# One-hot matrices turned by one product and two activations, and a target's scores taken in one product of 12 columns

## The chip, the cores and the metric

The kernel runs on one core of one Trainium2 chip. The metric is the device time of one execution, in microseconds (us); shorter is better. It is written by hand with a tile framework that allocates buffers, sets semaphores and orders the instructions of each engine.

## The reference

A graph of 6250 nodes with 256 features and 100,000 edges (`src`, `dst`, sorted by `dst`) passes through four layers of message passing. After each there is a residual addition and a layer norm.

```python
x = _layernorm(x + _L0_gnn_ref(x, ...))   # mean over incoming edges of relu(norm(x))[src]; two 256x256 products
x = _layernorm(x + _L1_gnn_ref(x, ...))   # 8-head attention: softmax over the edges of one src of q[src].k[dst], sum of v[dst]
x = _layernorm(x + _L2_gnn_ref(x, ...))   # two GAT layers, 4 heads of 64, below; gelu after each
x = _layernorm(x + _L3_gnn_ref(x, ...))   # mean over incoming edges of x[src]; three products
...
# one GAT layer
h = (h_in @ W).reshape(n, Hh, Cc)
alpha_s = jnp.sum(h * a_s, axis=-1)
alpha_d = jnp.sum(h * a_d, axis=-1)
e = jax.nn.leaky_relu(alpha_s[src] + alpha_d[dst], 0.2)
m = jax.lax.stop_gradient(jax.ops.segment_max(e, dst, num_segments=n))
ex = jnp.exp(e - m[dst])
alpha = ex / jax.ops.segment_sum(ex, dst, num_segments=n)[dst]
out = jax.ops.segment_sum(h[src] * alpha[:, :, None], dst, num_segments=n)
```

In the third step each node also has an edge to itself. A value that belongs to an edge's target, such as `alpha_d[dst]`, has to be brought from the node to each of its edges; the sums go the other way, from the edges to the node.

## The kernel before, in words

**Tiling.** The nodes are cut into `NB` = 50 blocks of `B` = 125. The edges of a block are laid in a list of up to `CAP` = 2048 places, 16 columns (`CM`) of 128 edges; what doesn't fit goes to two more columns (`SH`) that ten blocks (`GB`) share. For each place there is the number of the node at the far end (`idx_d`, `idx_s`) and a key, the place of the near node in its block (`key_d` for lists by target, `key_s` for lists by source). Both lie with the 128 edges of a column on the partitions. The lists by target are made first by `by_target` (L928), from the sorted `dst`; those by source by `by_source` (L1257), in small steps beside the first layer.

**A pass.** Each layer is a pass over pieces: a piece is four columns of one block (six in the first and last layer). For each column `gather` (L881) issues one indirect DMA on the POOL queue, which fetches 128 rows of a table in DRAM into the tile `g`. The sum over the edges of a node is a product on PE: the one-hot matrix `st` (128 edges by 125 nodes, made by VectorE in `one_hots`, L886, by comparing keys with `iota_p`) times the messages (L1755, L1955, L911).

**Where the change sits.** To bring a value from node to edge the turned matrix `ts` (125 nodes by 128 edges) is wanted as PE's stationary operand. `turned_hots` (L897) makes it: four transposes on PE of f32 (L901) into one PSUM tile `tp`, then one copy by ScalarE to bf16 (L903). Two passes use it:

- `piece1` (L1715), the attention pass over lists by source, 200 pieces: `ts` times the node's q, held as three bf16 parts, makes `qe` (L1739); VectorE multiplies it by the gathered k (L1742), sums over a head (`s`, L1687), ScalarE takes Exp (L1691, L1692), VectorE scales v into `msg` (L1694), PE adds into the block's sums `ps` (L1755).
- `piece2` (L1905), a GAT layer over lists by target, 200 pieces in each of two layers: `ts` times `ad_parts`, the node's four scores held as three bf16 parts, makes `pe` (L1922), three products of four columns for each of four columns of edges, added in PSUM. Then `messages` (L1880): VectorE adds gathered and own score (`e`, L1883), takes the leaky relu (`r`, L1877), ScalarE takes Exp (`pp`, L1886), VectorE makes `msg` (L1889), PE adds (L1955). Beside these pieces `count_edges` (L1780) builds a matrix of edge counts for the last layer, with VectorE (`a_hot`, L1804), PE (L1826) and ScalarE (`a_row`, L1813).

**Order of the work.** `run_pass` (L1490) starts one piece at each step and advances every piece that is under way by one `yield`, so about ten pieces are in flight, at different stages. After the last piece of a block `finish1` or `finish2` normalises, multiplies by weights, and writes the block's rows of the next layer's table on the SP queue (`move`, L795). The next pass's gathers read that table, so they start when all 50 blocks have been written: there is a seam between each two passes. `g` has 7 buffers in the attention pass and 9 in the GAT layers; `ts` 3, `msg` 3, `pe` and `pp` one each; `tp` one in the attention pass and two in the GAT layers. Engines run their queues in order; the framework sets the order from the order in which the code issues, its own estimates and free buffers. Only in the first stage, up to the writing of `h_table_f` (L1104), is the order on VectorE, ScalarE, POOL and SP that of the code (`manual_schedule`).

Of the kernel before, what the change touches and what calls it, by code (L numbers as in the profile page):

```python
# [7 lines left out]
F32 = mybir.dt.float32  # L8
I32 = mybir.dt.int32
F16 = mybir.dt.float16  # L10
BF16 = mybir.dt.bfloat16
AF = mybir.ActivationFunctionType
ALU = mybir.AluOpType
AX = mybir.AxisListType
ENG = mybir.EngineType

P = 128
# [638 lines left out]
def gnn_stack_kernel(ctx: ExitStack, tc: tile.TileContext, ins, out):  # L656
# [13 lines left out]
    nc = tc.nc  # L670
# [4 lines left out]
    B = max(p for p in range(1, P + 1) if N % p == 0)  # L675
    NB = N // B
    CM, SH = -(-E // (NB * P)), 2
# [4 lines left out]
    CAP = CM * P  # L682
# [19 lines left out]
    for c in range(EC):  # L702
        g = c // GQ
# [12 lines left out]
    for r in range(NR):  # L716
# [4 lines left out]
        c0 = max(0, int(place_of(g0 * GQ * EQ, -1)) // P) if g0 else 0  # L721
# [18 lines left out]
    with ExitStack() as fast:  # L740
        const = fast.enter_context(tc.tile_pool(name="fconst", bufs=1))
        dram = fast.enter_context(tc.tile_pool(name="fdram", bufs=1, space=bass.MemoryType.DRAM))
# [5 lines left out]
        pidx = const.tile([P, 1], F32, name="pidx")  # L748
        nc.gpsimd.iota(pidx, pattern=[[1, 1]], base=0, channel_multiplier=1, allow_small_or_imprecise_dtypes=True)
        ident = const.tile([P, P], F32, name="ident")  # L750
        nc.vector.tensor_scalar(ident, diff, 0.0, None, op0=ALU.is_equal)
        ones = const.tile([P, P], F32, name="ones")
        nc.vector.memset(ones, 1.0)
        ident_b = const.tile([P, P], BF16, name="ident_b")
# [24 lines left out]

        edge_rows = dram.tile([ER, P], I32, name="edge_rows_f")  # L780
        q_table = dram.tile([N, 3 * D], BF16, name="q_table_f")
        kv_table = dram.tile([N, 2 * D], F32, name="kv_table_f")
# [113 lines left out]

        def turned_hots(work, psum, st, n, bufs):  # L897

            tp = psum.tile([B, 4, P], F32, name="tp", bufs=bufs)
            for i in range(n):  # L900
                nc.tensor.transpose(tp[:, i, :], st[:, i, :], ident)  # L901
            ts = work.tile([B, 4, P], BF16, name="ts", bufs=3)
            nc.scalar.copy(ts[:, :n, :], tp[:, :n, :])  # L903
            return ts
# [23 lines left out]
        def by_target(pool, psum):  # L928
# [69 lines left out]
            for v, o in ((f, idx_d), (k_f, key_d)):  # L998
                for c0 in range(0, CM, 10):
# [4 lines left out]
                    nc.scalar.copy(o[:, :, c0 : c0 + n], pt[:, :n, :].rearrange("p i b -> p b i"))  # L1004
            yield
            p_row = psum.tile([1, NB + 1], F32, name="p_row")
            nc.tensor.transpose(p_row, row, ident[: NB + 1, : NB + 1])
# [635 lines left out]
        with tc.tile_pool(name="f1g", bufs=7) as gp, tc.tile_pool(name="f1", bufs=1) as pool, tc.tile_pool(  # L1643
# [71 lines left out]
            def piece1(b, c0, n):  # L1715
# [14 lines left out]
                yield  # L1730
                ts = turned_hots(work, psum, st, n, 1)
                yield
# [26 lines left out]
                if c0 + n == CM:  # L1759
                    del held[b]  # L1760
                    yield
                    yield from finish1(b)


# [72 lines left out]
        for layer in range(2):  # L1837
            table = hs_tables[layer]
            with tc.tile_pool(name=f"f2{layer}", bufs=1) as pool, tc.tile_pool(
# [5 lines left out]
                w_gat = gat_weight(pool, work, 1) if layer == 0 else None  # L1845
                sums, held, shared, late = {}, {}, {}, []

                def finish2(b):
# [56 lines left out]
                def piece2(b, c0, n):  # L1905
# [10 lines left out]
                    yield  # L1916
                    ts = turned_hots(work, psum, st, n, 2)
                    yield
                    pe = psum.tile([P, 4, H2], F32, name="pe")
                    for i in range(n):  # L1920
                        for k in range(3):
                            nc.tensor.matmul(  # L1922
                                pe[:, i, :], ts[:, i, :], ad_parts[:, b, k, :], start=(k == 0), stop=(k == 2)
                            )
                    yield
                    msg = work.tile([P, 4 * H2, C2 + 1], F32, name="msg", bufs=3)
                    steps = messages(g, n, pe[:, :n, :], msg)
                    next(steps)
# [238 lines left out]
```

## Time and profile before

| what | value |
|---|---|
| time, median of 3 runs | 7063.73 us (7057.86 to 7067.16) |
| the profiled execution's own time | 5192.17 us |
| its span | 5190.3 us |
| mean granted TensorE clock | 0.931 |
| busy PE / VectorE / ScalarE / POOL | 80% / 70% / 39% / 72% |
| gathers of the five passes | 800, 800, 800 + 800, 544 |
| first layer (lists made, h_table_f gathered) | 0 to 1249 us |
| attention pass, first to last gather of kv_table_f | 1235 to 2287 us |
| two GAT layers, first to last gather of hs_table_f | 2371 to 4450 us |
| last layer, from its first gather | 4474 to 5190 us |

A profile is one execution recorded by the hardware. Its own time lies well under the times of the runs that were not profiled, while span and own time agree; durations below are those of the profile. PE is TensorE's products, PEld its loads of the stationary operand, DVE is VectorE, ACT ScalarE, POOL GpSimd (here it issues the gathers), SP the queue of the plain DMAs. A group's line gives the source line, engine, operation, output and inputs, shapes and count; then the busy time in us and the mean of one in ns; then the idle time of the engine just before, with what ended most of it. "issue" is idle time that no recorded wait explains.

### The profile page before, as it was taken

Reading aid. Unit: us, or ns where it says so; the run is one execution under the profiler, and the core shown is the slowest. Engines: PE = TensorE matmul, PEld = TensorE weight load, DVE = VectorE, ACT = ScalarE, POOL = GpSimd, SP = SyncE. Lnnn points to the kernel's source line nnn. Section 1 sums busy time; section 2 is a strip of 40 time slices with the busy share of each in tenths; the row PEclk is TensorE's granted clock in tenths of the full one; section 3 lists DMA queues with packets and bytes.
Section 4 is the critical chain, followed back from the end, with each engine's and each line's share of the span. In section 5 each row is a group of like instructions: output and inputs, shape, how many; then the busy total and the mean of one; then the engine's idle time right before and its main releaser. Section 6 shows DMA issues by size and latency. Waiting matters only on the chain. (4 is left out here: it accounts for less than half of the span.)

```text
span 5190.3 us, 84722 instructions
## 1 busy us (share of the span) xinstructions
PE 4167.6 (80%) x27626; PEld 3130.5 (60%) x27626; DVE 3645.6 (70%) x11269; ACT 2029.7 (39%) x5923; POOL 3762.6 (72%) x3889
## 2 busy tenths in 40 slices
PE   0457999997999999976887888877777777799996
PEld 0245667665777777754666666655556656466664
DVE  7576788765999999975666666657777777423434
ACT  4011898895222222222444444434444444211212
POOL 6677677766777777745777777767777777677776
PEclk9877899998999999987999999989989899899998
DMA  4556677666777777753544444444444444788875
GB/s 132 147 156 175 174 194 191 187 171 189 224 224 227 224 224 227 225 148 101 136 131 131 133 131 137 131 114 135 133 133 136 135 136 134 201 244 245 246 208 144
DMA packets 365014, 883.97 MB, mean 170 GB/s; under 512 B 83596, under 2 KB 181954, under 8 KB 364562
## 3 DMA queue, kind: packets, MB, share of 16 engines
q0 software_dynamic: 232032, 702.40, 49.3%
q1 hardware_dynamic: 132530, 176.06, 11.5%
q8 instruction: 220, 3.60, 0.3%
q14 instruction: 232, 1.90, 0.1%
HBM read 791.50 MB, written 86.63 MB: 169 GB/s over the span
## 5 line engine op out<-in xcount | busy, mean ns | idle before, releaser
L882 POOL DMA_INDIRECT g<-hs_table_f,idx_d x1600 | 1528.8, 956 | 487.3 <-issue 424.0
L882 POOL DMA_INDIRECT g<-h_table_f,idx_d x800 | 795.6, 994 | 297.8 <-issue 210.8
L1955 PE MATMUL ps<-msg,st 128*125 128x260 f32 x3200 | 875.6, 417 | 83.4 <-DVE msg L1889 45.6
L882 POOL DMA_INDIRECT g<-kv_table_f,idx_s x784 | 744.0, 949 | 250.6 <-issue 184.6
L911 PE MATMUL ps<-g,st 128*128 128x256 bf16 (+1 forms) x4032 | 634.8, 282 | 201.1 <-DMA g<-h_table_f,idx_d 98.0
L1955 PEld LDWEIGHTS ps<-msg,st 128*125 128x125 f32 x3200 | 635.8, 204 | 232.6 <-issue 50.1
L882 POOL DMA_INDIRECT g<-x_table_f,idx_d x544 | 516.0, 949 | 189.1 <-issue 152.9
L903 ACT CAST ts<-tp 125x512 bf16<-125x512 f32 x600 | 347.5, 579 | 728.0 <-PE tp L901 709.9
L911 PEld LDWEIGHTS <-st 128*128 128x128 bf16 x4536 | 444.9, 101 | 295.5 <-issue 190.1
L1889 DVE TENSOR_TENSOR msg<-g,pp 128x1024 f32<-128x1024 f32 x400 | 485.3, 1213 | 19.7 <-ACT pp L1886 18.3
L1883 DVE TENSOR_TENSOR e<-g,pe 128x16 f32<-128x16 f32 x400 | 68.3, 171 | 607.3 <-DMA g<-hs_table_f,idx_d 419.6
L1755 PE MATMUL ps<-msg,st 128*125 128x264 f32 x1600 | 406.5, 396 | 51.1 <-DVE ln_t L825 12.9
L891 DVE TENSOR_TENSOR st<-iota_p,key_d 128x500 f32<-128x500 f32 (+1 forms) x550 | 410.0, 746 | 44.7 <-PE ps L911 27.0
L1922 PEld LDWEIGHTS <-ts 125*128 125x128 bf16 x4800 | 178.0, 97 | 430.7 <-issue 333.9
L1922 PE MATMUL pe<-ad_parts,ts 125*128 125x4 bf16 x4800 | 178.2, 165 | 320.3 <-DVE e L1883 255.5
L901 PE MATMUL tp<-ident,st 128*125 128x128 f32 x2400 | 405.5, 292 | 35.2 <-DVE st L891 16.1
L901 PEld LDWEIGHTS tp<-ident,st 128*125 128x125 f32 x2400 | 343.8, 197 | 67.1 <-issue 25.9
L1755 PEld LDWEIGHTS ps<-msg,st 128*125 128x125 f32 x1600 | 288.4, 190 | 113.9 <-issue 41.7
L1826 PE MATMUL a_acc<-a_hot,a_st 128*128 128x500 f16 x950 | 300.1, 403 | 38.7 <-ACT a_row L1813 28.0
L1739 PE MATMUL qe<-q,ts 125*128 125x256 bf16 x2400 | 311.2, 274 | 21.7 <-DVE prod L1742 9.9
L1438 ACT ACTIVATE oa<-o,blk 125x128 f16<-125x128 f16 x800 | 312.2, 391 | 38.9 <-PE acc L1445 28.6
L1804 DVE TENSOR_SCALAR a_hot<-a_nodes,a_ends 128x500 f16<-128x500 f16 x950 | 321.0, 364 | 1.9 <-PE a_acc L1826 1.4
(428 smaller groups left out, 8229.4 us busy)
## 6 DMA issues: line engine op xcount, KB each, us to landing
g<-hs_table_f,idx_d POOLq DMA_INDIRECT x1600
a_table_f<-a_row SPq DMA_DIRECT2D x50, 437.5 KB
cnt<-a_table_f SPq DMA_DIRECT2D x50, 437.5 KB
xs<-x_table_f SPq DMA_DIRECT2D x50, 336.0 KB
g<-h_table_f,idx_d POOLq DMA_INDIRECT x800
g<-kv_table_f,idx_s POOLq DMA_INDIRECT x784
hs_table_f<-hs SPq DMA_DIRECT2D x100, 115.5 KB
own<-hs_table_f SPq DMA_DIRECT2D x100, 115.5 KB
```

Of the source, the lines that this page charges most:

```text
L882: nc.gpsimd.indirect_dma_start(out=g, out_offset=None, in_=table, in_offset=bass.IndirectOffsetOnAxis(ap=idx, axis=0))
L891: nc.vector.tensor_tensor(st, iota_p[:, None, :w].to_broadcast([P, n, w]), key[:, :, None].to_broadcast([P, n, w]), op=ALU.is_equal,)
L901: nc.tensor.transpose(tp[:, i, :], st[:, i, :], ident)
L903: nc.scalar.copy(ts[:, :n, :], tp[:, :n, :])
L911: nc.tensor.matmul(ps[:, :m], st[:, i, :], g[:, i, k * D : k * D + m], start=(c0 + i == 0 and k == 2), stop=(c0 + i == CH - 1 and k == 0),)
L1438: nc.scalar.activation(oa, o1, AF.Copy, scale=val_a[:, at])
L1739: nc.tensor.matmul(qe[:, i, :], ts[:, i0 + i, :], q[:, k * D : (k + 1) * D], start=(k == 0), stop=(k == 2))
L1755: nc.tensor.matmul(sums[b], hot, m[:, i * H1 : (i + 1) * H1, :].rearrange("p h c -> p (h c)"), start=(c == 0), stop=(c == CH - 1),)
L1804: nc.vector.tensor_scalar(hots[k][:, i, :], nodes[:, r * RW : (r + 1) * RW], ends[:, s, c : c + 1], None, op0=ALU.is_equal,)
L1889: nc.vector.tensor_mul(msg[:, : n * H2, :C2].rearrange("p (n h) c -> p n h c", h=H2), g[:, :n, :D].rearrange("p n (h c) -> p n h c", h=H2) ...
L1922: nc.tensor.matmul(pe[:, i, :], ts[:, i, :], ad_parts[:, b, k, :], start=(k == 0), stop=(k == 2))
L1955: nc.tensor.matmul(sums[b][:B, : D + H2], hot, m[:, i * H2 : (i + 1) * H2, :].rearrange("p h c -> p (h c)"), start=False, stop=(c == CH - 1),)
```

## The change

`turned_hots` no longer transposes `st`. The keys of a block's list, 2048 in a row, are kept as one row of a tile `rows` (50 blocks by 2048, bf16). One bf16 product with a column of the identity, repeated 128 times as stationary operand, copies row `b` to all partitions (128 by 512, f32 in PSUM). ScalarE then takes Abs of key minus partition number (into `off`, bf16) and Relu of 1 minus that: 1 where the key is the partition's number, else 0. The keys by target are rounded to bf16 in `by_target` and written to a table `key_rows_f` in DRAM, which each GAT layer loads; the keys by source are transposed from `key_s` at the start of the attention pass. And in `piece2` the three parts of the scores are taken by one product of 12 columns, after which VectorE sums the parts into a tile `ad`.

```diff
--- before.py
+++ after.py
@@ -747,6 +747,8 @@
         nc.gpsimd.iota(iota, pattern=[[1, P]], base=0, channel_multiplier=0, allow_small_or_imprecise_dtypes=True)
         pidx = const.tile([P, 1], F32, name="pidx")
         nc.gpsimd.iota(pidx, pattern=[[1, 1]], base=0, channel_multiplier=1, allow_small_or_imprecise_dtypes=True)
+        minus = const.tile([P, 1], F32, name="minus")
+        nc.vector.tensor_scalar(minus, pidx, -1.0, None, op0=ALU.mult)
         ident = const.tile([P, P], F32, name="ident")
         nc.vector.tensor_scalar(ident, diff, 0.0, None, op0=ALU.is_equal)
         ones = const.tile([P, P], F32, name="ones")
@@ -778,6 +780,7 @@
         h_table = dram.tile([N, 3 * D + 2], BF16, name="h_table_f")
         edge_rows = dram.tile([ER, P], I32, name="edge_rows_f")
+        key_rows = dram.tile([NB, CAP], BF16, name="key_rows_f")
         q_table = dram.tile([N, 3 * D], BF16, name="q_table_f")
         kv_table = dram.tile([N, 2 * D], F32, name="kv_table_f")
         hs_tables = [dram.tile([N, D + 8], F32, name=f"hs_table_f{i}") for i in range(2)]
@@ -894,13 +897,19 @@
             )
             return st
-        def turned_hots(work, psum, st, n, bufs):
-            tp = psum.tile([B, 4, P], F32, name="tp", bufs=bufs)
-            for i in range(n):
-                nc.tensor.transpose(tp[:, i, :], st[:, i, :], ident)
+        def turned_hots(work, psum, rows, b, c0, n, bufs):
+            tp = psum.tile([P, 512], F32, name="tp", bufs=bufs)[:, : n * P]
+            nc.tensor.matmul(
+                tp, ident_b[:NB, b : b + 1].to_broadcast([NB, P]), rows[:, c0 * P : (c0 + n) * P], start=True, stop=True
+            )
+            off = work.tile([B, 4 * P], BF16, name="off")[:, : n * P]
+            nc.scalar.activation(off, tp[:B], AF.Abs, bias=minus[:B, :])
             ts = work.tile([B, 4, P], BF16, name="ts", bufs=3)
-            nc.scalar.copy(ts[:, :n, :], tp[:, :n, :])
+            nc.scalar.activation(
+                ts[:, :n, :].rearrange("p n e -> p (n e)"), off, AF.Relu, scale=-1.0, bias=ones[:B, 0:1]
+            )
             return ts
         def add_rows(ps, st, g, c0, n, more=0):
@@ -1003,6 +1012,10 @@
                         nc.tensor.transpose(pt[:, i, :], v[:, (c0 + i) * P : (c0 + i + 1) * P], ident[:NB, :NB])
                     nc.scalar.copy(o[:, :, c0 : c0 + n], pt[:, :n, :].rearrange("p i b -> p b i"))
             yield
+            rounded = half.bitcast(BF16)[:, :CAP]
+            nc.scalar.copy(rounded, k_f)
+            nc.sync.dma_start(out=key_rows[:, :], in_=rounded)
             p_row = psum.tile([1, NB + 1], F32, name="p_row")
             nc.tensor.transpose(p_row, row, ident[: NB + 1, : NB + 1])
@@ -1728,7 +1741,7 @@
                         gather(g[:, i, :], kv_table[:, :], idx_s[:, b, c0 + i : c0 + i + 1])
                 st = one_hots(work, key_s[:, b, c0 : c0 + n], n, 4, 6)
                 yield
-                ts = turned_hots(work, psum, st, n, 1)
+                ts = turned_hots(work, psum, rows, b, c0, n, 1)
                 yield
                 prod = work.tile([P, 4, D], F32, name="prod")
                 for i0 in range(0, n, 2):
@@ -1760,6 +1773,14 @@
                     del held[b]
                     yield
                     yield from finish1(b)
+            rows = pool.tile([NB, CAP], BF16, name="rows")
+            for c0 in range(0, CM, 4):
+                n = min(4, CM - c0)
+                tp = psum.tile([P, 512], F32, name="tp")[:NB, : n * P]
+                for i in range(n):
+                    nc.tensor.transpose(tp[:, i * P : (i + 1) * P], key_s[:, :, c0 + i], ident)
+                nc.scalar.copy(rows[:, c0 * P : (c0 + n) * P], tp)
             each = len(made) // NB
@@ -1844,6 +1865,8 @@
                 bias = load_row(pool, ins[f"L2_gnn_b{layer}"], "bias")
                 w_gat = gat_weight(pool, work, 1) if layer == 0 else None
                 sums, held, shared, late = {}, {}, {}, []
+                rows = pool.tile([NB, CAP], BF16, name="rows")
+                nc.sync.dma_start(out=rows, in_=key_rows[:, :])
                 def finish2(b):
                     whole = sums.pop(b)
@@ -1914,17 +1937,19 @@
                         gather(g[:, i, :], table[:, :], idx_d[:, b, c0 + i : c0 + i + 1])
                     st = one_hots(work, key_d[:, b, c0 : c0 + n], n, 4, 6)
                     yield
-                    ts = turned_hots(work, psum, st, n, 2)
+                    ts = turned_hots(work, psum, rows, b, c0, n, 2)
                     yield
-                    pe = psum.tile([P, 4, H2], F32, name="pe")
+                    pe = psum.tile([P, 4, 3, H2], F32, name="pe")
                     for i in range(n):
-                        for k in range(3):
-                            nc.tensor.matmul(
-                                pe[:, i, :], ts[:, i, :], ad_parts[:, b, k, :], start=(k == 0), stop=(k == 2)
-                            )
+                        nc.tensor.matmul(
+                            pe[:, i].rearrange("p k h -> p (k h)"), ts[:, i, :],
+                            ad_parts[:, b].rearrange("p k h -> p (k h)"), start=True, stop=True,
+                        )
                     yield
+                    ad = work.tile([P, 4, H2], F32, name="ad")
+                    nc.vector.tensor_reduce(ad[:, :n, :], pe[:, :n].rearrange("p n k h -> p n h k"), AX.X, ALU.add)
                     msg = work.tile([P, 4 * H2, C2 + 1], F32, name="msg", bufs=3)
-                    steps = messages(g, n, pe[:, :n, :], msg)
+                    steps = messages(g, n, ad[:, :n, :], msg)
                     next(steps)
                     if c0 == 0:
```

## The prediction, made before the change was run

> **What bounds the kernel now.** I read busy shares and slices of the page first, then the groups, POOL's waits, and the engines in windows that lie well inside the three passes that the change touches.
>
> ```profile
> PE 4167.6 (80%) x27626; PEld 3130.5 (60%) x27626; DVE 3645.6 (70%) x11269; ACT 2029.7 (39%) x5923; POOL 3762.6 (72%) x3889
> POOL 6677677766777777745777777767777777677776
> ```
>
> PE has the largest share, POOL only 72%. But POOL stands at 7 tenths nearly from end to end, a plateau. The windows give the level: attention pass, first GAT layer, second.
>
> ```profile
> core 0: us, PE busy (x) PEld busy (x) DVE busy (x) ACT busy (x) POOL busy (x), PEclk, DMA share, GB/s
> 1320.00:2240.00 920.00, 844.41 (x5052) 672.78 (x5051) 893.90 (x2044) 253.32 (x806) 696.39 (x735) 0.99 0.77 226
> 2420.00:3380.00 960.00, 772.81 (x5489) 603.62 (x5487) 620.99 (x1702) 400.01 (x1133) 727.43 (x764) 0.93 0.49 132
> 3500.00:4380.00 880.00, 671.62 (x4738) 517.51 (x4738) 655.48 (x2358) 387.02 (x987) 667.72 (x698) 0.92 0.49 135
> ```
>
> 920/735, 960/764 and 880/698 are 1.25, 1.26 and 1.26 us for one gather, in passes that load PE, DVE and the DMA engines quite differently. What is the quarter in which POOL isn't busy?
>
> ```profile
> POOL g L882 <- issue: 977.2, 3208, 0.3
> POOL gs L882 <- DVE st L891: 79.3, 1, 79.3
> POOL g L882 <- PE acc L1445: 48.6, 56, 11.4
> POOL gs L882 <- DMA hs_table_f<-hs: 18.7, 1, 18.7
> POOL g L882 <- DMA kv_table_f<-kv: 12.4, 2, 12.1
> ```
>
> The columns are us in all, times, longest. 977 us are gaps of 0.30 us with no recorded wait, one after nearly each gather: 0.95 + 0.30 = 1.25, a full queue. The waits that count are single ones at seams (79, 19, 12 us), where the next table must be complete (the first is put down to `st`, but what is late there is the last write of hs_table_f). 3744 main gathers x 1.25 = 4680 of 5190 us. So in the profile the pacer is POOL's issue, and other engines count only at seams or when they make POOL wait. Two reserves are small: in the attention pass DVE is 97% and PE 92% busy (893.90/920, 844.41/920).
>
> **What the skill says.** (1) Perfetto Trace Analysis, the section on the DMA instruction of SWDGE: the recorded end of a GpSimd DMA is when its descriptors are written, not when data has moved; and under "What 'DMA-bound' means", a solid issuing track is a bound of its own. The trace agrees: a solid track at 226 and at 132 GB/s alike. (2) ScalarE: Activation LUTs, "What ACT_TABLE_LOAD costs": about 280 ns + 0.833 ns per element with one bias operand, and 93 for each further one. The trace agrees: the x_sb activation, 256 elements with bias and scale operands, takes 597 ns, where this gives 586. (3) The same page, "Table sets": relu and abs stand in every set, so they ask for no load. This trace has no Abs in it. (4) TensorE: Matmul & The Clock Gate, "Back-to-back issue gap": N/2.4 + 2.5 ns, 216 ns for 512 columns. The trace agrees: three products of 500 columns at 3386.27 us take 0.80 us where one alone takes 0.37, so 0.215 each more.
>
> **The change part by part.** A piece lasts four gathers and its share of the shared ones, about 5.0 us.
>
> ```profile
> L903 ACT CAST ts<-tp 125x512 bf16<-125x512 f32 x600 | 347.5, 579 | 728.0 <-PE tp L901 709.9
> L1883 DVE TENSOR_TENSOR e<-g,pe 128x16 f32<-128x16 f32 x400 | 68.3, 171 | 607.3 <-DMA g<-hs_table_f,idx_d 419.6
> L1922 PE MATMUL pe<-ad_parts,ts 125*128 125x4 bf16 x4800 | 178.2, 165 | 320.3 <-DVE e L1883 255.5
> L901 PE MATMUL tp<-ident,st 128*125 128x128 f32 x2400 | 405.5, 292 | 35.2 <-DVE st L891 16.1
> ```
>
> *Turned matrix, PE.* Four transposes hold PE for 405.5/600 = 0.68 us a piece. One product of 512 columns in a stream takes about 0.22, with its load up to 0.25. Saved: 0.43 x 600 = 258 us. *Scores, PE.* Twelve small products take 178.2/400 = 0.45 us; their time is that of loads and starts, 0.037 each, so four of 12 columns take 0.15. Saved: 0.30 x 400 = 120 us. Together 378 of PE's 4168 us, none on the path: PE has 115 to 208 us idle in each window and POOL waits for none of it inside a pass. If POOL were not the pacer, this would be the gain.
>
> *ScalarE.* The copy of 0.579 becomes Abs and Relu. A bias operand costs half of 597 - 417 (x_sb against Gelu, 256 columns each), 0.09; reading SBUF in place of PSUM some 0.05 (417 against 366 for the aT copy). Abs 0.67, Relu 0.72: +0.81 us a piece, 486 us in all; the skill's price, 2 x 0.706, gives +0.83. ScalarE goes from 1.38 to 2.2 us a piece in the attention pass, and from 387/(698/4) = 2.2 to 3.0 in a GAT layer, of 5.0. Hidden. Behind them in ScalarE's queue stands the Exp `pp`, for which DVE's `msg` waits; see the slower rival.
>
> *DVE.* The sum of three parts, 48 values per partition from PSUM, is new: 400 times. Its bounds are the smallest such rows, 0.15, and `s`, 1206 ns for 1024, which leaves about 0.25 for 48; I take 0.20, 80 us in all. `e` then reads SBUF, 0.02 less. DVE is 65% and 74% busy there: hidden. It also changes a wait: `pe` has one buffer and was held until `e`, which waits for gathered rows; that is how PE waits 255.5 us for `e`. Now the sum frees `pe` without the gather, so PE gets ahead. Below nothing this can bring the seam behind each layer nearer, 0 to 10 us each, since PE has less left over; I take 0, because what is late there is the last gather's landing and the chain through Gelu, w_gat and the write.
>
> *Start.* ScalarE's rounding of 50x2048 costs what the cast of that shape before it does, 1.90 us (100.20 us), ahead of the copy `ends_sb`, for which DVE waits (126.69 us) and behind it the start of `by_source`. The DMA of `key_rows_f` goes on SP behind the writes of h_table_f and ahead of the weights, about 1 us of issue; the first gather follows the last of these. Bounds 0 and 4 us; I take 2.
>
> *Keys by source.* Sixteen transposes of 128x50, four copies of up to 50x512, one `tp` buffer, hence four rounds of 0.7 + 0.6 + 0.3 us of hops: 6 us between the freeing of the buffers (first transpose before: 1282.4 us) and the first product of the pass. POOL is then issuing; it stops only if the 7 buffers of `g` fill. From 1234.8 to 1303 us it issues about 45 gathers with the shared ones, close to full as the first `msg` frees one. Bounds 0 and 6; I take 2.
>
> *Rows for GAT layers.* One DMA each on SP, in the place of the bias load and ahead of the loads of `own`; 0.4 us of issue, landing under the first gathers, whose rows take over 2 us. 0 to 2 us a layer; I take 0.
>
> Sum: -378 of PE, +486 of ScalarE, +80 of DVE hidden; +4 us on the path (range -20 to +16). The profiled execution goes from 5192.17 to about 5196.
>
> **From there to the median.** The runs' median is 7063.73, 1871 us or 36% above the profiled execution, and no view shows why. If every one of 3889 POOL instructions took 0.48 us more (1871/3889), it would fit, and POOL would pace even more. A fixed addition would also leave the difference alone. If PE were held at the rate of the idle seam (four f32 products of w_gat take 2.12 us at 2314 us against 1.16 at 2303, 1.83 times) PE alone would need 7600, more than the median: so not that as such, but something between isn't excluded. I carry the 4 us over: **7068**.
>
> **The rivals.**
> *PE paces the unprofiled runs (15%).* For it: the 36%, and PE's largest share. Against it: the profile's plateau. The 378 us, stretched by 7064/5190 = 1.36, are 514: 6550 us.
> *Seams shorten (8%).* `pe` freed early and less PE work bring three seams 10 us each nearer, and the queue at the end of the attention pass drains sooner: 7035.
> *Slower: Exp behind Abs and Relu in the second GAT layer (22%).* DVE is idle 880 - 655 = 225 us over 174.5 pieces, 1.29 us a piece, less 0.18 for the new sum. If Abs and Relu of a later piece stand ahead of `pp`, `msg` comes up to 1.39 later, in DVE's ordered queue. It decides once more than 1.11 us a piece is lost so; paid in full it makes 0.28 x 200 = 56 us, with the start 7125. Now `msg` waits for `pp` only 18.3 us in 400 pieces, and ScalarE has other work between: so not likely, but DVE's ordered queue is where the new latency would show. In the attention pass DVE has 0.14 us a piece to spare; there too the price would come.
> *The new functions switch tables (3%).* 1283 ns twice a piece, as Gelu and Exp pay once a block: ScalarE at 3.0 + 2.6 = 5.6 us passes the pace of 5.0 by 0.6 in 400 pieces: 7300.
> That the change isn't in effect I leave out; the instructions named are replaced.
>
> **How the numbers follow.** The pacer holds with 52%: 7068, its own range 7050 to 7095. A difference below 0.2%, 14 us, is about what a measurement can't tell from none. Of the main case's 52 points I put 33 within that, 15 above (the planner orders every queue anew, and the start and the keys can cost their upper bounds) and 4 below. Of the seams' 8, 2 are within; of the first slower rival's 22, 4. Faster: 15 + 6 + 4 = 0.25. Same: 33 + 2 + 4 = 0.39. Slower: 15 + 18 + 3 = 0.36. The range takes in shortened seams and the slower rival with some more for a piece order that I can't see, and leaves out PE as pacer and table loads: 6980 to 7160.
>
> **What would show it.** Right: gathers still 1.25 us apart in all three passes, POOL's waits inside a pass still short, PE's busy time near 3790, ScalarE's near 2515, DVE's near 3725, seams at the same distance within 5 us. The product of 512 columns near 0.22 us in a stream, Abs and Relu near 0.7 each, no more table loads than about 200. Wrong: gaps in POOL ended by `msg` or `prod` (buffers of `g` full), `msg` waiting for `pp` much over 18 us, a first gather of the attention pass later than 1240 us; or a median that moves by hundreds of us while the profile's span stands still, which would mean that unprofiled runs have another bound.

## The result and the profile after

| | median | runs |
|---|---|---|
| before | 7065.44 us | 4, 7057.86 to 7073.03 |
| changed | 7139.05 us | 4, 7134.56 to 7151.69 |

The ratio is 1.0107, with a 95% interval of 1.0089 to 1.0125: the changed kernel is slower by 1.1%, 74 us. That lies within the range of 6980 to 7160, but on the other side of the likeliest case (7068, no change), and close to the first slower rival (7125).

The profiled execution of the changed kernel took 7134.56 us, with a span of 7132.8, like its other runs; the execution of the kernel before on which the prediction was built (5192) was not a usual one, and a second profile of that kernel (e1, below) took 6942 us. The three parts of the page that the prediction began with, first of the changed kernel:

```profile
PE 4566.2 (64%) x22642; PEld 3022.6 (42%) x22642; DVE 3709.6 (52%) x11670; ACT 2490.3 (35%) x6528; POOL 3754.9 (53%) x3889
...
POOL 5664444443555555552555555555555555366664
PEclk9777888877788888886777777777776777788987
```

The same lines of e1, the kernel before in a usual execution:

```profile
PE 4640.6 (67%) x27626; PEld 3386.6 (49%) x27626; DVE 3657.6 (53%) x11269; ACT 2048.3 (30%) x5923; POOL 3739.0 (54%) x3889
...
POOL 5664544444555555553555555545555555366664
PEclk9677888877888888886788888877777778789998
```

POOL's plateau of 7 tenths has become one of 5, in both. The windows of the changed kernel inside the attention pass and the two GAT layers (columns as in the prediction):

```profile
1900.00:3100.00 1200.00, 852.92 (x4107) 596.03 (x4105) 827.57 (x1885) 353.56 (x902) 640.55 (x675) 0.85 0.55 159
3450.00:4600.00 1150.00, 694.45 (x2965) 458.76 (x2964) 555.70 (x1635) 460.28 (x1131) 631.78 (x662) 0.76 0.35 96
4850.00:6100.00 1250.00, 744.64 (x2964) 457.44 (x2965) 690.35 (x2593) 510.77 (x1193) 680.80 (x714) 0.73 0.36 97
```

A gather now takes 1200/675 = 1.78, 1.74 and 1.75 us, not 1.25. POOL's waits say why (us in all, times, longest):

```profile
POOL g L885 <- issue: 1019.7, 3258, 3.2
POOL g L885 <- PE acc L1458: 388.3, 50, 33.5
POOL g L885 <- DVE msg L1912: 373.5, 62, 12.2
POOL g L885 <- PE ps L920: 207.1, 63, 13.9
POOL g L885 <- DVE msg L1707: 198.3, 47, 7.0
```

The short gaps of 0.3 us are still there, but beside them POOL now waits 1267 us for VectorE and 640 for PE (the sums of all such lines, these among them; 196 and 67 in the profile of the prediction). Where the line ends at `msg`, no buffer of `g` is free, because `msg` comes late. This is what the prediction named as proof against itself. But it isn't the change that brought these waits: in e1 they are 1235 and 576 us. The groups that were changed:

```profile
L910 ACT ACTIVATE ts<-off,ones 125x512 bf16<-125x512 bf16 x600 | 429.7, 720 | 1465.7 <-remote 1042.7
...
L908 ACT ACTIVATE off<-tp,minus 125x512 bf16<-125x512 f32 x600 | 405.1, 682 | 568.2 <-remote 422.2
...
L904 PE MATMUL tp<-rows,ident_b 50*128 50x512 bf16 x600 | 270.5, 467 | 424.8 <-ACT off L908 379.6
...
L1944 PE MATMUL pe<-ad_parts,ts 125*128 125x12 bf16 x1600 | 104.2, 173 | 634.8 <-DVE ad L1950 230.1
```

The same places in e1:

```profile
L903 ACT CAST ts<-tp 125x512 bf16<-125x512 f32 x600 | 349.7, 583 | 2349.8 <-remote 1413.0 <-PE tp L901 494.2 <-issue 141.9
...
L901 PE MATMUL tp<-ident,st 128*125 128x128 f32 x2400 | 450.6, 314 | 59.6 <-issue 16.5 <-DVE st L891 14.6 <-ACT ts L903 14.5
```

Abs and Relu last what was forecast (0.68 and 0.72; 0.67 and 0.72). ScalarE stands 1466 us ahead of Relu and 568 ahead of Abs, mostly for something marked "remote", a releaser that the trace doesn't show. Together that is 2034 us, less than the 2350 that it stood ahead of the one copy in e1. What is new is that PE stands 425 us ahead of `tp`, 380 of them for Abs to free its buffer; in e1 it was 60.

### The profile page after: what moved, and what is told of

It reads as the page before. It is cut to its first block, busy times and chain, and to the rows that moved or that the text cites. A ratio compares the mean times of both kernels' runs of the same rounds, so it can differ in the third digit from the quotient of the medians.

```text
span 7132.8 us, 75552 instructions
## 1 busy us (share of the span) xinstructions
PE 4566.2 (64%) x22642; PEld 3022.6 (42%) x22642; DVE 3709.6 (52%) x11670; ACT 2490.3 (35%) x6528; POOL 3754.9 (53%) x3889
## 4 chain that ended last, share of the span: by engine, by line
PE 37%; another core or an unknown queue 26%; DVE 12%; issue 11%; ACT 9%; POOL 4%; DMA 2%; SPq 0%; DVEq 0%; ACTq 0%; POOLq 0%
PE ps L1980 6%; PE ps L920 5%; PE acc L1458 4%; PE d L2112 4%; PE pt L881 3%; PE po L881 3%; POOL g L885 3%; PE ps L1768 3%; PE qe L1752 3%; ACT ts L910 2%; DVE msg L1912 2%; ACT off L908 2%; PE a_acc L1847 2%; DVE st L894 2%
## 5 line engine op out<-in xcount | busy, mean ns | idle before, releaser
L1980 PE MATMUL ps<-msg,st 128*125 128x260 f32 x3200 | 1034.3, 475 | 77.9 <-DVE msg L1912 53.7
L910 ACT ACTIVATE ts<-off,ones 125x512 bf16<-125x512 bf16 x600 | 429.7, 720 | 1465.7 <-remote 1042.7
L1980 PEld LDWEIGHTS ps<-msg,st 128*125 128x125 f32 x3200 | 728.7, 236 | 373.3 <-DVE msg L1912 81.9
L908 ACT ACTIVATE off<-tp,minus 125x512 bf16<-125x512 f32 x600 | 405.1, 682 | 568.2 <-remote 422.2
L904 PE MATMUL tp<-rows,ident_b 50*128 50x512 bf16 x600 | 270.5, 467 | 424.8 <-ACT off L908 379.6
L1912 DVE TENSOR_TENSOR msg<-g,pp 128x1024 f32<-128x1024 f32 x400 | 485.9, 1215 | 90.8 <-ACT pp L1909 43.9
L1944 PE MATMUL pe<-ad_parts,ts 125*128 125x12 bf16 x1600 | 104.2, 173 | 634.8 <-DVE ad L1950 230.1
L1447 DVE TENSOR_SCALAR oh<-iota_h,ups 125x300 f16<-125x300 f16 (+4 forms) x800 | 233.1, 299 | 474.4 <-PE acc L1458 289.2
L1944 PEld LDWEIGHTS <-ts 125*128 125x128 bf16 x1600 | 101.2, 104 | 775.1 <-issue 373.6
L1752 PE MATMUL qe<-q,ts 125*128 125x256 bf16 x2400 | 374.8, 306 | 81.7 <-DVE prod L1755 67.2
L1755 DVE TENSOR_TENSOR prod<-g,qe 128x512 f32<-128x512 f32 x400 | 269.3, 682 | 280.0 <-remote 250.3
L1752 PEld LDWEIGHTS <-ts 125*128 125x128 bf16 x2400 | 252.7, 109 | 344.4 <-issue 281.0
```

The costliest lines, as they stand in the source:

```text
L908: nc.scalar.activation(off, tp[:B], AF.Abs, bias=minus[:B, :])
L910: nc.scalar.activation(ts[:, :n, :].rearrange("p n e -> p (n e)"), off, AF.Relu, scale=-1.0, bias=ones[:B, 0:1])
L1752: nc.tensor.matmul(qe[:, i, :], ts[:, i0 + i, :], q[:, k * D : (k + 1) * D], start=(k == 0), stop=(k == 2))
L1912: nc.vector.tensor_mul(msg[:, : n * H2, :C2].rearrange("p (n h) c -> p n h c", h=H2), g[:, :n, :D].rearrange("p n (h c) -> p n h c", h=H2) ...
L1980: nc.tensor.matmul(sums[b][:B, : D + H2], hot, m[:, i * H2 : (i + 1) * H2, :].rearrange("p h c -> p (h c)"), start=False, stop=(c == CH - 1),)
```

## What a usual execution looks like

A stretch of e1 in the attention pass, lines in order of time (start, duration, engine, line, in brackets the idle time before):

```profile
2411.67 0.67 PE L901 MATMUL tp<-ident,st 128*125 128x128 f32 x4
...
2412.70 1.21 DVE L1687 TENSOR_REDUCE s<-prod 128x32 f32<-128x1024 f32 x1
...
2412.86 2.02 PE L1755 MATMUL ps<-msg,st 128*125 128x264 f32 x8 [0.52 <-DVE ln_t L825]
...
2417.22 0.94 POOL L882 DMA_INDIRECT g<-kv_table_f,idx_s  x1 [0.30 <-issue]
2420.52 0.69 DVE L1742 TENSOR_TENSOR prod<-g,qe 128x512 f32<-128x512 f32 x1 [6.54 <-remote]
2420.65 0.58 ACT L903 CAST ts<-tp 125x512 bf16<-125x512 f32 x1 [11.04 <-remote]
...
2421.13 0.21 ACT L1691 ACTIVATE pp<-s 128x32 f32<-128x32 f32 x1
```

By the trace PE has finished `tp` at 2412.34 us, yet ScalarE's copy of it starts at 2420.65 and VectorE's product with `qe` at 2420.52, nearly at one moment. The records of the semaphores (counters by which one engine tells another that it is done) show why: PE's last three instructions that carry a signal end at 2411.07, 2411.73 and 2412.34, and the next three arrivals are at 2420.49, 2420.57 and 2420.63, 8 to 9 us later. The ends of products are modelled in such a trace, so it could be that PE itself stood; but three instructions that end 0.6 us apart signal within 0.14 us, so it looks like signals held back, not like work done late. Meanwhile POOL goes on gathering until it has no buffer left, and in this stretch the signals arrive as the last gathered rows land. And Exp, `pp`, whose input `s` was ready at 2413.92, waits until 2421.13 in ScalarE's queue, behind the copy.

I measured this in every trace: the time from the end of the last PE instruction that carries a signal to the signal's recorded arrival. In the profile that the prediction used, 5144 of 5146 recorded PE signals come within 0.1 us. In e1 1166 of 4612 come more than 1 us late, in the changed kernel 1042 of 4449; of VectorE's and ScalarE's in e1, 2 each (in no run over 17). The table gives the time in which a PE signal was over 1 us late (overlaps counted once, unrecorded signals missing, so a lower bound); how long Exp waited, from the end of its input `s` or `r` to its start, summed over 205 Exps each in the attention pass and the two GAT layers; and VectorE's idle time that ScalarE ended.

| | ratio to before, 95% | PE signals late, us | Exp waits, us | VectorE on ScalarE, us |
|---|---|---|---|---|
| before, profile of the prediction | | 6 | 50, 93, 186 | 131 |
| e1, before again | | 1978 | 450, 240, 495 | 405 |
| changed | 1.0107 (1.0089 to 1.0125) | 1974 | 536, 511, 795 | 589 |
| e2, scores only | 1.0036 (1.0023 to 1.0049) | 2056 | 457, 472, 583 | 595 |
| e3, turned only | 1.0082 (1.0057 to 1.0107) | 1862 | 520, 293, 637 | 541 |
| e4, comparison on VectorE | 0.9785 (0.9754 to 0.9816) | 1720 | 144, 339, 198 | 265 |
| e5, copy on VectorE | 1.0058 (1.0036 to 1.0080) | 1933 | 207, 241, 245 | 246 |
| e6, comparison, three products | 0.9882 (0.9854 to 0.9910) | 2007 | 146, 360, 231 | 238 |
| e7, pause after each gather | 1.0360 (1.0337 to 1.0382) | 1219 | 64, 149, 358 | 298 |
| e8, fewer g | 0.9950 (0.9935 to 0.9965) | 2001 | 441, 225, 485 | 407 |
| e9, two copies | 1.0004 (0.9992 to 1.0017) | 2051 | 563, 279, 531 | 481 |
| e11, sum twice | 1.0032 (1.0019 to 1.0045) | 1855 | 533, 535, 514 | 462 |
| e12, comparison and pause | 1.0020 (1.0005 to 1.0034) | 1802 | 223, 355, 210 | 475 |

The 1978 us of late signals are of the size of what was missing: 6940 - 5190 = 1750 us. The DMA engines don't explain it: the packets of the gather queue took 49.3% of 5190 us and 36.4% of 6940 us, 2.56 and 2.53 ms. Nor does POOL's work, 3763 and 3739 us. That the late signals are the cause of the long time rests on these two traces. Between the other rows the sums don't rank the kernels: e2's Exp waits more than e3's (1512 us in all against 1450) and it costs less.

## The experiments

Each ran beside the kernel before on its own chip: e1 to e4 where before has a median of 6946 us, e5 to e8 at 6955, e9 to e12 at 7058. Ratios compare across these, times don't. The changed kernel itself was timed beside a kernel before of 7065 us and on none of these chips; how far a ratio moves from chip to chip was not measured, so a difference of some tenths of a per cent between ratios of different chips is uncertain.

**e1** is the kernel before, unchanged.

> The kernel before, unchanged, for a second profile of it. If the long time of the plain runs is a condition in which this kernel usually runs, this profile shows about 7065 us, POOL well under 72% busy and a granted clock near 0.79, as the changed kernel's profile does. If recording is what shortens the execution, it shows about 5192 us and a clock near 0.93 again.

It took 6942 us, with a clock of 0.82 and POOL at 54%: the long time is its usual one, recorded or not. The prediction's base was the exception.

**e2, e3: one half of the change each.** e2 has the hunks for `pe`, `ad` and `messages` alone, e3 all others.

In e2, against before:

```diff
+                    pe = psum.tile([P, 4, 3, H2], F32, name="pe")
...
+                            pe[:, i].rearrange("p k h -> p (k h)"), ts[:, i, :],
...
+                    nc.vector.tensor_reduce(ad[:, :n, :], pe[:, :n].rearrange("p n k h -> p n h k"), AX.X, ALU.add)
```

In e3, against the changed kernel:

```diff
-                            pe[:, i].rearrange("p k h -> p (k h)"), ts[:, i, :],
...
+                                pe[:, i, :], ts[:, i, :], ad_parts[:, b, k, :], start=(k == 0), stop=(k == 2)
...
-                    nc.vector.tensor_reduce(ad[:, :n, :], pe[:, :n].rearrange("p n k h -> p n h k"), AX.X, ALU.add)
```

> Only the product of 12 columns and the sum of three parts; the matrices are turned by transposes and one copy as before. If VectorE's sum or its place in VectorE's queue is the cost, this carries most of it: 7110 to 7140 us. If the cost is ScalarE's two activations, this is no slower than before, and up to 30 us faster since 120 us of PE go: 7035 to 7068. If the cost is fixed work at the start and at the rows, 7065 within 10.

> Only the matrices made by Abs and Relu from the repeated row; the three products for a target's scores as before. If Abs and Relu on ScalarE are the cost, this takes all of it and perhaps more than the changed kernel, for lack of the shorter product: 7130 to 7170 us. If VectorE's sum is the cost, about 7065 or, with 258 us of PE gone, below it.

Measured: 6970 us, 1.0036, and 7009 us, 1.0082. Two thirds of the price go with the turned matrices, a third with the scores; 0.36 + 0.82 = 1.18% agrees with the whole's 1.07. Neither half gains although both take work from PE. e2 fits none of its three expectations; e3 comes near the first, that Abs and Relu are most of the cost.

**e4: the comparison on VectorE**, in the changed kernel:

```diff
-            off = work.tile([B, 4 * P], BF16, name="off")[:, : n * P]
-            nc.scalar.activation(off, tp[:B], AF.Abs, bias=minus[:B, :])
...
+            nc.vector.tensor_scalar(
+                ts[:, :n, :].rearrange("p n e -> p (n e)"), tp[:B], pidx[:B, :], None, op0=ALU.is_equal
+            )
```

> The changed kernel with one comparison on VectorE (is the repeated key this partition's index?) in the place of Abs and Relu. If ScalarE's two activations and the hop between them are the cost, it falls away, and some 0.6 us a piece comes on VectorE: 7040 to 7100 us. If what counts is VectorE's ordered queue, where the comparison now waits for PE, it is slower than the changed kernel: 7180 us or more. If the cost is fixed work (keys by source, rows), about 7139 us.

Measured: 6795 us, 0.9785. It beats both kernels, before by 2.1%, and every expectation. The comparison takes 0.74 us, as long as Abs or Relu, and VectorE is busier by 411 us than in e1 (4068.4 against 3657.6):

```profile
PE 4556.2 (67%) x22642; PEld 2970.7 (44%) x22642; DVE 4068.4 (60%) x12270; ACT 1771.2 (26%) x5328; POOL 3754.4 (55%) x3889
...
L908 DVE TENSOR_SCALAR ts<-tp,pidx 125x512 bf16<-125x512 f32 x600 | 445.7, 743 | 93.4 <-remote 69.2
```

Exp's waits fall from e1's 1185 us to 681, and ahead of `ts` its engine stands 93 us. PE's idle time ahead of `tp` falls too, from the changed kernel's 425 us to 61.

**e5: is it the engine alone?** The kernel before, with its copy on VectorE.

```diff
-            nc.scalar.copy(ts[:, :n, :], tp[:, :n, :])
+            nc.vector.tensor_copy(ts[:, :n, :], tp[:, :n, :])
```

> The kernel before with one edit: the copy of the four transposed matrices out of PSUM runs on VectorE instead of ScalarE. Theory (what counts is that ScalarE's queue stands at ts, waiting for PE's signal, with the Exp behind it): this gains as the comparison on VectorE did, 2% or more, about 0.975 to 0.985 of before. Rival (the comparison gained because the product of 512 columns takes 0.4 us less of PE than four transposes): no gain here, 1.000 to 1.010 with 0.5 us a piece more on VectorE.

Measured: 6987 us, 1.0058. My theory that only ScalarE's queue counts fell, and the rival's number came true. Exp's waits are as short as in e4 (693 us), but now VectorE stands for PE's signal:

```profile
L903 DVE CAST ts<-tp 125x512 bf16<-125x512 f32 x600 | 412.0, 687 | 417.2 <-remote 187.7 <-PE pe L1922 103.1 <-PE tp L901 81.3
```

417 us against 93 in e4. A transpose can only start when VectorE has made `st`; the product of the repeated key needs nothing of VectorE, and PE can do it ahead of time, so that its signal is there when VectorE comes to it. The product of the repeated key with the comparison is worth 1.0058 - 0.9882 = 1.8% over transposes with a copy, from e5 to e6, on one chip. Two things differ between these: the early signal, and 0.3 us less of PE a piece (427.5 against 260.1 us in all). No run parts them; e3, which has the same product and gains nothing, speaks against PE's time alone.

**e6: comparison on VectorE, three products**, that is e3 with e4's edit.

> The comparison on VectorE from the repeated key's row, but with the three products for a target's scores as before and no sum on VectorE. Theory (each part has its own price, as the two halves alone cost 24 and 63 us): the sum's 0.4% is saved on top, about 0.974 of before. Rival (in company with the comparison the shorter product pays): slower than the comparison with the product of 12 columns, above 0.979.

Measured: 6869 us, 0.9882. The rival holds: in company with the comparison the product of 12 columns gains 1% (e4's ratio against e6's, on two chips whose kernel before takes 6946 and 6955 us), where alone (e2) it costs 0.4%. The parts have no prices of their own.

**e7: a looser stream of gathers**, in the kernel before.

```diff
+        rest = const.tile([P, 400], F32, name="rest_f")
...
+            nc.gpsimd.memset(rest, 0.0)
```

> The kernel before with a memset of 128x400 on POOL behind every gather, some 0.4 us each. Theory (PE's signals are held back while gathered rows land without a break, and come through when the landings stop): the looser stream lets signals through, fewer and shorter holds, POOL's waits shrink by more than the 1500 us that the memsets add is worth: 6300 to 6900 us. Rival (POOL's own issue time counts in full, as the prediction had it): 1500 us are added where POOL runs, 7600 us or more. A third: the memsets fill POOL's waits and nothing changes, 6950 within 50.

```profile
PE 4742.6 (66%) x27626; PEld 3430.2 (47%) x27626; DVE 3716.7 (51%) x11269; ACT 2071.9 (29%) x5923; POOL 5250.8 (73%) x7739
...
L886 POOL MEMSET rest_f<- 128x400 f32 x3298 | 1447.4, 439 | 155.8
```

(In the last layer a name clash makes the memset one of 128x2, 0.1 us.) Measured: 7206 us, 1.036. None of the three as written: POOL works 1512 us more than in e1, the kernel is slower by 251 only. In the attention pass late signals fall from 446 us to 43, in the whole from e1's 1978 to 1219 (2001 in e8, on the same chip as e7). In the first GAT layer they fall from 493 to 234, in the second only from 506 to 423. So the late signals do hang on the stream of gathers; but the breaks cost 251 us more than they bring.

**e8: fewer buffers of g**, in the kernel before: 4 for 7 and 5 for 9.

> The kernel before with 4 instead of 7 buffers of g in the attention pass, and 5 instead of 9 in the GAT layers. Theory (a held signal comes through when POOL has filled every free buffer): holds become shorter in proportion, from a mean of some 5 us to 3, and more frequent; the time changes by less than 2% either way, holds per pass up by a third or more. Rival (holds have nothing to do with POOL's gathers): holds keep length and number, and with less fetched ahead the kernel is slower by over 3%.

Measured: 6914 us, 0.995. Late signals stay (443 stretches, 2001 us, against 435 and 1978), so they don't last longer with more buffers: the theory is wrong, though the time changed by less than 2%. Of the rival the first half holds, holds of the same length and number; the second, a kernel slower by over 3%, doesn't.

**e9: a second ScalarE step alone**, in the kernel before.

```diff
+            off = work.tile([B, 4, P], BF16, name="off")
+            nc.scalar.copy(off[:, :n, :], tp[:, :n, :])
-            nc.scalar.copy(ts[:, :n, :], tp[:, :n, :])
+            nc.scalar.copy(ts[:, :n, :], off[:, :n, :])
```

> The kernel before with one more copy on ScalarE: PSUM to a bf16 tile, and that to ts; nothing else is touched, PE keeps its four transposes. Theory (a second ScalarE step between PE's signal and ts costs part of its length, and in the changed kernel PE's saving hid that): 0.55 us and a hop a piece, against 0.81 for Abs and Relu, slower by 1.2 to 2.4%, 1.012 to 1.024 of before. The prediction's view (ScalarE has time to spare, hidden): 1.000 within 0.003. If it shows about 1.008, as the turned matrices alone did, PE's saving is worth nothing.

Measured: 7061 us, 1.0004. The prediction's view holds here: ScalarE's time is hidden, and 0.6 us more a piece cost nothing. So a second ScalarE step of Abs's or Relu's size doesn't cost by its length. What differs is where the steps stand. e9's two steps:

```profile
L905 ACT COPY ts<-off 125x512 bf16<-125x512 bf16 x600 | 368.2, 615 | 13.2 <-PE qe L1741 2.9
...
L904 ACT CAST off<-tp 125x512 bf16<-125x512 f32 x600 | 348.8, 582 | 2122.2 <-remote 1397.7 <-PE tp L901 429.0 <-issue 97.7
```

The second follows the first at once (13 us of idle time ahead of it in all), and all the standing, 2122 us, is ahead of the first. In the changed kernel it is split, 568 us ahead of Abs and 1466 ahead of Relu, but in sum not longer. And PE stands 89 us ahead of `tp` here, 425 in the changed kernel.

**e10: one ScalarE step after the product**, the changed kernel without Abs, so that the scores are others.

> The changed kernel without Abs: ts is Relu of one minus the repeated key, straight from PSUM, one ScalarE step as before; so ts marks only keys of 0 and the scores aren't those of the reference. Theory (PE's saving is worth about 1.8%, the second ScalarE step takes it back): 0.980 to 0.995 of before. Rival (PE's saving is worth nothing, the cost lies in the sum or in fixed work): 1.003 to 1.011.

It took 20,243 us and tells nothing: with those scores the kernel ran its general path too, as lines that the fast path hasn't show (13,264 executions of L361).

**e11: the sum done twice**, in the changed kernel: the `tensor_reduce` into `ad` stands there two times.

> The changed kernel with VectorE's sum of three parts done twice, 0.20 us more in 400 pieces, 80 us in all. If the sum counts in full: 1.022 of before. If VectorE's time counts in part, as ScalarE's seems to (a third): 1.014. If it is hidden: 1.011, as the changed kernel.

Measured: 7085 us, 1.0032. None of the three: with more work the ratio is lower than the changed kernel's, measured on another chip. Exp's waits in the second GAT layer are 514 us instead of 795, and VectorE's idle time on ScalarE 462 instead of 589. So 80 us more of VectorE's work don't show. It may be that below one per cent the order in which engines meet late signals counts for more than the work; or the two chips differ.

**e12: e4 with pauses**, 128x128 on POOL behind each gather from the attention pass to the second GAT layer.

> The comparison on VectorE and the product of 12 columns, with a memset of 128x128 on POOL behind every gather of the attention pass and the GAT layers (some 0.2 us, about 480 us in all). Theory (pauses in the gather stream let PE's signals through): holds in these passes fall by a third or more and pay for part of the pauses; below 0.979 of before only if they pay in full, else 0.98 to 1.00. Rival (the pauses add up): 0.979 plus 480 us, 1.045.

Measured: 7068 us, 1.002: 2.4% slower than e4's ratio. It lies between the two expectations. Late signals (1802 us against 1720) don't fall, so here the pauses only cost. Of the kernels tried, e4 is the best.

## Why the prediction was right or wrong

**The range held, by luck.** 7139 us lies between 6980 and 7160, but not by the reasoning of the main case: its pacer wasn't there in the runs, and a slowdown of 1.1% wasn't what it forecast. The nearest was the first slower rival, at 22%.

**The base: wrong, and the step that failed.** "A fixed addition would also leave the difference alone ... I carry the 4 us over." What lay between 5192 and 7064 us was no fixed addition, and not POOL's own pace either: in e1, a usual execution, PE's signals arrive late and POOL waits for buffers, so POOL's issue no longer paces. With it fell that "the pacer is POOL's issue": 1.75 us a gather, not 1.25. The text named the gap of 36% and that no view explained it; it should have lowered the main case for that, as every "hidden" in the sum leaned on a pacer seen in one execution.

**ScalarE +486: right in size, and hidden as work.** 405.1 + 429.7 - 349.7 = 485 us; e9 shows that 0.6 us of such work a piece, three quarters of it, costs nothing. **VectorE +80: right**, 80.9 us in `ad`.

**PE -378: half wrong.** Against e1, `tp` fell from 450.6 to 270.5 us and `pe` from 183.8 to 104.2, 260 in all: the product of 512 columns took 0.45 us, not 0.25. The price in a stream didn't apply: one such product took 386 ns (median of 361) at full clock and 583 (of 239) at half clock. A reading was off too, though nothing hangs on it: PE's idle time in the windows was 76 us at the least (920.00 - 844.41), not 115.

PE's busy time as a whole, on one chip, fell only from 4640.6 to 4556.2 (e4), since the rest took longer: `ps<-msg,st`, 4800 products as before, 1417 us in e1 and 1504 in e4.

The Trainium skill, TensorE: Matmul & The Clock Gate, "Part 1: The HAM clock gate", says that PE falls to half its clock after an idle window of about 3.4 us. This case agrees in part: the granted clock is 1.0 or 0.5 in steps of 3.41 us; in e1, 152 of the 171 gaps of PE over 4 us have such a fall inside them or in the window behind. But the idle window need not be empty: of e1's 305 falls only 78 came behind a window of 3.41 us in which PE did as good as nothing (under 2% busy), and 293 behind one in which it was busy for less than half; of the 945 other windows at full clock only 25 were busy for less than half. So a late signal can be paid twice. PE stood at half clock for 720 us in the profile of the prediction, 2515 in e1 and 2984 in the changed kernel. That less work on PE leaves more idle windows fits this, but no run isolates it.

**Start, keys by source, table loads: nothing against them.** The first gather is at 147 us as before; the attention pass's first comes at 1709 us, and at 1711 in e9, which has the start of the kernel before, on a chip of like speed. But single profiles of kernels with that start differ by up to 17 us on one chip (1681 in e5, 1698 in e8), so the 4 us can't be told. ScalarE loads its tables 202 times, as before.

**The slower rival: its mechanism is seen, but not shown to be the cause.** "If Abs and Relu of a later piece stand ahead of `pp`, `msg` comes up to 1.39 later, in DVE's ordered queue." In the changed kernel, second GAT layer:

```profile
5528.54 0.16 DVE L1900 SCALAR_TENSOR_TENSOR r<-e 128x16 f32<-128x16 f32 x1
...
5531.92 0.94 POOL L885 DMA_INDIRECT g<-hs_table_f,idx_d  x1 [0.30 <-issue]
5535.77 0.72 ACT L910 ACTIVATE ts<-off,ones 125x512 bf16<-125x512 bf16 x1 [8.07 <-remote]
5536.39 0.57 ACT L1834 ACTIVATE a_row<-a_acc 125x500 bf16<-125x500 f32 x1
...
5537.25 0.19 ACT L1909 ACTIVATE pp<-r 128x16 f32<-128x16 f32 x1
5537.38 0.43 DVE L838 TENSOR_TENSOR xp<-x_r,xp 125x256 bf16<-125x256 f32 x1 [6.96 <-ACT xp L837]
...
5539.68 1.22 DVE L1912 TENSOR_TENSOR msg<-g,pp 128x1024 f32<-128x1024 f32 x1
```

`r` is ready at 5528.70; Relu starts at 5535.77, just after one of PE's signals arrives, at 5535.74 (the last `pe` before it ended at 5525.56); Exp comes 8.55 us after its input, and VectorE idles 6.96 for `xp`, another step of ScalarE behind Relu. In this stretch it isn't the length of Abs and Relu (1.39 us) that is lost, as the rival reckoned, but the late signal in front of Relu. And it doesn't show where I said to look, at `msg` waiting for `pp` (43.9 us after, 89.0 in e1), since VectorE is stopped earlier in its queue.

Against e9, as fast as before and on a chip of like speed, Exp waits 1842 us instead of 1373, with all of the difference in the GAT layers; VectorE stands 108 us more for ScalarE; the two layers' time is 70 us longer (1444.5 + 1474.3 against 1418.9 + 1429.7); the kernel, 78. On one chip it looks otherwise: from e1 to e3 the first gather of the attention pass comes 10.5 us later, the time from there to the first GAT layer's first gather grows by 37 (1567 to 1604), and the two GAT layers together by 26 (2834.2 to 2860.7). Both compare single profiles.

**What is shown and what isn't.** Shown: the price is there with either half, it isn't the length of the ScalarE work (e9), a longer sum adds none (e11), and it turns into a gain when the repeated key is compared on VectorE (e4, e6). Argued from traces only: that Relu's stand for a free `ts` is the cause. Against it: ScalarE stood longer ahead of `ts` in e1, and Exp waits more in e2, which has no Relu, than in e3. A rival is PE's own ordered queue. In the three kernels with Abs and Relu PE stands ahead of `tp`, mostly for Abs to free its buffer, 425 us (changed), 578 (e3) and 510 (e11), in all others of the table 17 to 120. More buffers of `ts`, or of `tp` and `off`, in the changed kernel would test the two; that was not tried. So which wait makes the 1.1% stays open. Open too: why PE's signals come late in the usual executions and did not in the one of 5192 us.

## What to carry to other kernels

When a profiled execution and the runs differ by a third, get a second profile before pricing anything: "hidden" is a statement about a pacer, and the pacer was another. Where a producer's signal can be late, a consumer that stands for it in an ordered queue can hold up everything queued behind it. Try such waits on the engine whose next work needs that signal anyway, with the producer's work issued early, as the comparison on VectorE did; moving the wait alone (e5) didn't pay. Nor did taking work from PE by itself (e2, e3).

## What the runs showed of the hardware

- PE's signals were late, hardly any others: in e1 1166 of 4612 recorded ones by more than 1 us, 23 of them by more than 12; of ScalarE's and VectorE's 2 each. A pause of 0.44 us a gather took the late time of the attention pass from 446 us to 43. In the stretch above they came through as the stream of gathers broke off (2420.5 us), but that isn't a rule: half a us after the first of a run of late signals in e1 the gather queue was empty in 49% of 530 cases, at random times in 42%.
- PE's granted clock fell behind windows of 3.41 us in which PE was busy for less than half (293 of e1's 305 falls), entirely idle or not.
- A comparison on VectorE of 125x512 from PSUM (f32 to bf16) took 743 ns, a copy 687; ScalarE's copy 583, Abs 682, Relu 720.
- Work can be added for nothing: a copy of 0.6 us a piece on ScalarE (1.0004), and a second sum on VectorE (1.0032 against the changed kernel's 1.0107, on different chips).
